# Moving softmax steps and weight preparation around two products with values in a gated cross-attention block

## The chip, the cores and the metric

The kernel runs on one core of one Trainium2 chip, in one launch. The metric is the time of the execution on the device in microseconds (us); of several executions the median is taken. Each core has a matrix engine (PE, with its weight loads shown apart as PEld), a vector engine (DVE), a scalar engine (ACT), a general engine (POOL), and a sync engine (SP), which here issues the DMA transfers. Each engine works through its own list of instructions in order, and waits at an instruction whose inputs or buffers are not ready.

## The reference

```
h   = layernorm(x)                           # x: 32 batches x 64 tokens x 512
q   = h   @ Wq ; k = ctx @ Wk ; v = ctx @ Wv # 32 heads of 128 columns each
s   = q k^T / sqrt(128) + bias               # per batch and head, 64 x 64
p   = softmax(where(mask, s, -inf)), 0 where masked
x   = x + tanh(g_xattn) * ((p v) @ Wo)
y   = layernorm(x) @ weight^T + bffn + (low-rank adapter of the batch's segment)
out = x + tanh(g_ffn) * y
```

All inputs and the output are 32-bit floats.

## The kernel before

**Precision.** A product of 32-bit matrices is made of three matmuls in a reduced 32-bit type: each operand is split into a high part (a cast on ACT) and a low part (the original minus the high part, a subtraction on DVE or POOL), and high x high, high x low and low x high are summed in PSUM (`mm3`, L94 to L100). Every operand of such a product therefore costs a cast and a subtraction before PE can take it. In the attention, `ch` and `cl` (for two of the pairs `cx`) are the high and low part of the context, the attention's weighted sum of values.

**Projections.** Keys, values and queries are made by `unit`: each operand is cut into 2 x 2 blocks and the product is done with seven block products instead of eight (Strassen's method in Winograd's form). The weights' sums of blocks and their splits are made ahead of time by `prep` (with `pair_blocks`). For one pair of heads `prep` has eight steps (the list `PREP`): four sums on POOL (`s1` to `s4`, L283), seven casts on ACT (`hp1` to `hp7`, L290), and seven subtractions on POOL (`lp1` to `lp7`, L294). With the last step it issues on SP the fetch of the next pair's raw weights into the one buffer `rawq` (L259), which has to wait until the last reader of that buffer, the subtraction `lp4`, is done.

**Stages.** The tokens are worked in two phases of 1024 (16 batches). Each phase first makes the keys and values of all heads and puts them into DRAM, and then goes through 16 pairs of heads, numbered n from 0 to 15. For each pair there are these steps, whose order `run` writes out by hand:

- `q_unit(n)`: the query projection, from the prepared weights of pair n.
- `score(n)`: `scores` makes both heads' scores (L861 on PE), adds the bias and takes the row maximum on DVE (L863, L865), subtracts it on POOL (L866), and leaves the exponential (L875) to ACT.
- the softmax's rest, in small steps: sums and reciprocals on DVE, the product with them on POOL (L888), a transpose of 32 x 32 blocks on DVE (`tp`, L899), and copies of these blocks to their places on ACT (L896; `pt`, for pair 14 `pz`). `turned` has them for one pair, `last_turned`, with 16 steps, for pairs 14 and 15 together. The mask is added to the bias ahead of time on POOL (L815).
- `pv(n)`: the product with the values (L1010 on PE) and the split of its result, for each of two heads in two halves: a cast on ACT (L1014) and a subtraction on DVE (L1015), four pairs of them in all.
- `oproj(n)` (for the last pairs `oproj2`): the product of the context with the output weights, `pa` on PE, added to `acc` on DVE (L1059). The output weights are fetched and split like the others (`start_o`, L91).

**What sets the order.** The schedule is manual: each engine gets its instructions in the order in which the program writes them. Everything that isn't a step of `run` is a generator in the list `streams`: the preparation of weights, the softmax's steps, the loads. A call of `beat()` advances every generator in the list by one step. Beats stand in the middle of the large steps: one after each of the seven block products of `unit`, one after each of the four casts and subtractions of `pv`, one after each head's scores, one after each of the eight tiles of `oproj`. So what is issued between two instructions of a large step depends on which generators are in the list at that time.

**Around the change.** Pair 0's product with values comes after `q_unit(1)`; the preparation of pair 2's query weights (`start_q(2)`) is put into the list just before it:

```
q_unit(1)
start_q(2)
pv(0)
score(1)
oproj(0)
q_unit(2)
```

Pair 13's product with values comes right after the scores of pairs 14 and 15, whose `last_turned` is then in the list. Its context goes to the buffers `cx`, and its output projection follows.

Of the kernel before, what the change touches and what calls it, by code (L numbers as in the profile page):

```python
# [27 lines left out]
NPR = H // 2  # L28
# [15 lines left out]
def flamingo_block(ctx: ExitStack, tc: tile.TileContext, x, xT, ctxT, bias, mask, gx, gf,  # L44
# [19 lines left out]
    def beat():  # L64
        for g in list(streams):
            if next(g, True):
                streams.remove(g)

    def drain(g):
        if g is not None and g in streams:  # L70
            streams.remove(g)
            for _ in g:
                pass
# [12 lines left out]
    def psum(name, shape=(P, 512)):  # L86
        return psp.tile(list(shape), F32, tag="ps", name=name)
# [166 lines left out]
    def fetch(kind, n, tag, pieces=1):  # L254
        raw = rwp.tile([P, 1024], F32, tag=tag, name=f"raw{kind}{n}")
        w = 1024 // pieces
        for i in range(pieces):
            sl = slice(i * w, (i + 1) * w)
            nc.sync.dma_start(out=raw[:, sl], in_={"k": wk, "q": wq, "o": wo}[kind][n % NPR][:, sl])  # L259
        raw_of[kind, n] = raw  # L260
# [39 lines left out]
    def prep(kind, n, eng, wait=0, at=0, then=None):  # L300
        for _ in range(wait if at == 0 else 0):
            yield
        do = pair_blocks(kind, n, eng)
        for k, ops in enumerate(PREP):
            if at and k == at:
                for _ in range(wait):
                    yield
            do(*ops)
            if then and k == len(PREP) - 1:
                then()  # L310
            yield
# [483 lines left out]
    def attention(p, res, rest, qt, freed):  # L795
# [6 lines left out]
        def load_v(n):  # L802
            b["v", n] = big(res[3 if n < NPR - 1 else 2], [P, NT, 256], F32, f"v{p}_{n}")
            nc.sync.dma_start(out=b["v", n], in_=vd[p][n // 2][:, :, n % 2 * 256:(n % 2 + 1) * 256])
# [177 lines left out]
        def ctx_of(n):  # L982
            if n in (NPR - 3, NPR - 1):
                if not more_ctx:
                    more_ctx.extend(big(qt[4 + k], [P, 2, TP], F32R, f"cx{p}_{k}") for k in range(2))
                return more_ctx
            return ch, cl

        def turn_pair(n, **pace):
            drain(b["n", n])  # L990
            b["s", n] = turned(n, **pace)
            next(b["s", n])
            next(b["s", n])

        def pv(n, cs=(0, 1)):
            drain(b["s", n])
            if n == NPR - 4:
                turn_pair(n + 1, pace=(0, 1, 2, 2, 3, 2, 2, 2, 2))
                next(b["s", n + 1])


            pt, v, (hi, lo) = pts[n == NPR - 2], b["v", n], ctx_of(n)
            ts = [c * 4 + t for c in cs for t in range(4)]
            for i in (1, 0) if n == 0 else (0, 1):
                ps = [psum(f"po{p}_{n}_{i}_{cs[0]}{h}", (P, len(ts), S)) for h in range(2)]
                for k, t in enumerate(ts):
                    for h in range(2):
                        keys = slice(h * S, (h + 1) * S)
                        for d in range(0, P, S):
                            nc.tensor.matmul(ps[h][d:d + S, k, :], v[keys, t, i * P + d:i * P + d + S],  # L1010
                                             pt[keys, i, t, :], start=True, stop=True)
                for h in range(2):
                    o, l = [x[:, i].rearrange("p (t h s) -> p h t s", h=2, s=S)[:, h, ts[0]:ts[-1] + 1] for x in (hi, lo)]
                    nc.scalar.copy(o, ps[h])  # L1014
                    nc.vector.tensor_tensor(l, ps[h], o.bitcast(F32), ALU.subtract)  # L1015
                    beat()
            if n + 1 < NPR - 1:
                load_v(n + 1)
                if ("n", n + 1) in b:
                    if n != NPR - 4:  # L1020
                        turn_pair(n + 1)
                    streams.append(b["s", n + 1])
# [69 lines left out]
        def run(xq, prefetch, before_last, last_unit, values_read, beside=None):  # L1092
            qb = {}


            def start_q(n, eng=nc.gpsimd, wait=0):
                g = p * NPR + n
                qb[n] = prep("q", g, eng, wait, then=(lambda: fetch("q", g + 1, "r0")) if n + 1 < NPR else None)
                streams.append(qb[n])

            def q_unit(n):
                g = p * NPR + n
                drain(qb.get(n))
                if n == 0:
                    start_q(1, nc.vector, 2)
                elif n == NPR - 1:
                    before_last()
                elif n % 2 == 0 or n == 3:
                    start_q(n + 1)
                qT[n] = kqp.tile([P, 2, TP], F32, tag="kq", name=f"qT{g}")  # L1110
                if n == 1:
                    start_o(0, 2)
                end = unit(wt[("q", g)], xq, None, k_dst(qT[n]), f"q{g}", tuple(carry))
                carry.clear()
                end()
                if n % 2 and 3 < n < NPR - 1:
                    start_q(n + 1)

            def score(*ns):
                for n in ns:  # L1120
                    drain(b.get(("m", n)))
                for n in ns:
                    for i in (0, 1) if n else (1, 0):
                        scores(n, i, qT[n], b["k", n])
                for n in ns:
                    if 0 < n < NPR - 2:
                        load_k(n + 2)
                n = ns[0]
                if n == 0:
                    b["s", n] = first_softmax()  # L1130
                elif n == NPR - 2:
                    b["s", n] = b["s", n + 1] = last_turned()
                else:
                    b["s", n] = both(normed(n, 1), turned(n))
                streams.append(b["s", n])
                if 1 < n < NPR - 2:
                    b["n", n + 1] = normed(n + 1, 5)
                    streams.append(b["n", n + 1])

            q_unit(0)  # L1140
            enter_late()
            b["m", 1] = bias_mask(1)
            score(0)
            streams.append(b["m", 1])
            streams.append(load_acc())
            q_unit(1)
            start_q(2)
            pv(0)
            score(1)
            oproj(0)  # L1150
            q_unit(2)
            start_o(1)
            pv(1)
            q_unit(3)
            score(2, 3)
            for a in range(4, NPR, 2):
                oproj(a - 3)
                q_unit(a)
                start_o(a - 2)
                pv(a - 2)  # L1160
                q_unit(a + 1)
                if a < NPR - 2:
                    oproj(a - 2)
                start_o(a - 1)
                if a < NPR - 2:
                    pv(a - 1)
                else:
                    drain(b["s", a - 1])
                    next(ob[a - 1])
                    held = list(streams)  # L1170
                    streams.clear()
                score(a, a + 1)
                if a == NPR - 8:
                    streams.append(paced(prefetch(), 4))

            n = NPR - 4
            load_v(n + 3)
            beat()
            streams.append(ob[n + 1])
            drain(ob[n + 1])  # L1180

            def between():
                pv(n + 1)
                streams.extend(g for g in held if g is not ob[n + 1])
                last_unit()
                start_o(n + 2, 3)

            def hold():
                drain(ob[n + 3])
                drain(b["s", n + 3])  # L1190
                held[:] = streams
                streams.clear()


            oproj2(n, [(0, 0), (0, 1), between, (0, 2), (0, 3), (1, 0), (1, 1), (1, 2), (1, 3),
                       lambda: start_o(n + 3, 3)]
                   + [(k, t) for t in range(4, NT - 1) for k in range(2)]
                   + [(0, NT - 1), hold, lambda: pv(n + 2), (1, NT - 1), lambda: pv(n + 3)])
            streams.extend(held)
            values_read(acc)  # L1200
            oproj2(n + 2, [(0, 0), (0, 1), (1, 0), (1, 1)] + [(k, t) for t in range(2, NT) for k in range(2)], beside)
# [263 lines left out]
```

## Time and profile before

| | |
|---|---|
| median of 3 runs | 1477.29 us (1476.85 to 1477.81) |
| the profiled execution's own time | 1477.5 us |
| its span in the profile | 1475.7 us |
| granted clock of PE | 1.0 |
| instructions | 31292 |
| PE busy | 99% of the span |
| POOL busy | 71% |
| DVE busy | 64% |
| ACT busy | 48% |
| mean traffic with memory | 176 GB/s |

The profile shows one execution. The shares are of the whole span, so they say which engine is always at work, and not where it waits. Waits are read from the list of what an engine waited for, and from the timeline, where each line is a run of like instructions: start, busy time, engine, line of the program, operation, what is written and read, and in brackets the idle time before it, with what ended it.

### The profile page before, as it was taken

What the parts mean: (1) busy time and instruction counts of PE and PEld (TensorE: products, weight loads), DVE (VectorE), ACT (ScalarE), POOL (GpSimd) and SP (SyncE); (2) the same over time, 40 slices, a digit from 0 to 9 for tenths busy, and PEclk for the clock granted to TensorE, in tenths of its full rate; (3) what the DMA queues carried; (4) which work ended last, traced back from release to release, by engine and by line L of the source; (5) the groups of instructions that cost most, each with busy time, mean ns of one, the idle gap of its engine ahead of it and who ended that gap; (6) DMA issues with size and microseconds to landing.
All of it is one profiled execution on the core that took longest, in us unless ns stands there. A gap on an engine that the chain in (4) does not pass through costs nothing.

```text
span 1475.7 us, 31292 instructions
## 1 busy us (share of the span) xinstructions
PE 1467.0 (99%) x12008; PEld 1220.4 (83%) x12008; DVE 940.2 (64%) x1589; ACT 714.6 (48%) x1582; POOL 1052.0 (71%) x1160
## 2 busy tenths in 40 slices
PE   9999999999999999999999999999999999999999
PEld 7888888888888888888888888888888888888887
DVE  5675464367675677576479756435767567757774
ACT  5444233346555665666334423334655665566611
POOL 4999378969767676767989938896875758577520
PEclk9999999999999999999999999999999999999999
DMA  5754554475443455353385765437545344625554
GB/s 194 287 204 164 179 179 174 143 261 185 152 168 106 168 180 208 101 186 109 127 294 203 235 226 186 173 136 260 184 152 178 103 170 170 217 93 184 136 127 131
DMA packets 148343, 259.38 MB, mean 176 GB/s; under 512 B 44417, under 2 KB 78209, under 8 KB 144098
## 3 DMA queue, kind: packets, MB, share of 16 engines
q1 hardware_dynamic: 147906, 256.87, 50.7%
q8 instruction: 94, 1.54, 0.4%
q10 hardware_dynamic: 288, 0.52, 0.1%
q14 instruction: 55, 0.45, 0.1%
HBM read 179.74 MB, written 77.61 MB: 174 GB/s over the span
## 4 chain that ended last, share of the span: by engine, by line
PE 97%; DVE 1%; issue 1%; ACT 1%; POOL 0%; DMA 0%; SPq 0%; DVEq 0%; POOLq 0%
PE pa L100 23%; PE pxq L100 6%; PE pvq L100 6%; PE pvv L100 6%; PE pxv L100 6%; PE pzv L100 6%; PE pzq L100 6%; PE pzk L100 6%; PE pvk L100 6%; PE pxk L100 6%; PE po L1010 4%; PE ps L861 4%; PE pf L100 3%; PE pyq L100 3%; PE pyv L100 3%; PE pyk L100 3%
## 5 line engine op out<-in xcount | busy, mean ns | idle before, releaser
L100 PE MATMUL pa<-wo,ch 128*128 128x512 f32 x896 | 278.2, 392 | 0.4 <-ACT ch L1014 0.4
L896 ACT COPY pt<-tp 32x256 f32<-32x256 f32 x452 | 182.4, 404 | 69.7 <-DVE tp L899 60.1
L100 PEld LDWEIGHTS pa<-wo,ch 128*128 128x128 f32 x896 | 166.6, 188 | 36.0 <-ACT ch L1014 0.7
L100 PE MATMUL pa<-wo,cl 128*128 128x512 f32 x448 | 174.1, 389 | 0.0
L1059 DVE TENSOR_TENSOR acc<-pa,acc 128x512 f32<-128x512 f32 x192 | 129.4, 681 | 53.5 <-PE pa L100 53.5
L815 POOL TENSOR_TENSOR sm<-sm,madd 128x512 f32<-128x512 f32 x60 | 77.2, 1295 | 96.5 <-DMA sm<-bias 96.5
L888 POOL TENSOR_TENSOR sm<-sm,r 128x512 f32<-128x512 f32 x64 | 66.8, 1044 | 72.5 <-DVE r L887 70.2
L351 DVE TENSOR_TENSOR vt<-pvv,vt 128x512 f32<-128x512 f32 x64 | 44.2, 691 | 103.1 <-PE pvv L100 103.1
L1015 DVE TENSOR_TENSOR cl<-po,ch 128x512 fp32r<-128x512 f32 x112 | 74.5, 689 | 47.6 <-ACT ch L1014 47.2
L100 PEld LDWEIGHTS pa<-wo,cl 128*128 128x128 f32 x448 | 84.1, 188 | 17.7
L866 POOL TENSOR_TENSOR sm<-sm,mx 128x512 f32<-128x512 f32 x64 | 67.0, 1050 | 34.9 <-DVE mx L865 34.7
L351 DVE TENSOR_TENSOR qT<-pvq,qT 128x512 f32<-128x512 f32 x64 | 44.1, 690 | 61.9 <-PE pvq L100 60.5
L373 ACT COPY vt<-pxv 128x512 f32<-128x512 f32 x32 | 18.8, 588 | 130.9 <-PE pxv L100 130.9
L875 ACT ACTIVATE sm<-sm 128x512 f32<-128x512 f32 x62 | 39.2, 633 | 78.0 <-POOL sm L866 78.0
L351 DVE TENSOR_TENSOR kT<-pvk,kT 128x512 f32<-128x512 f32 x60 | 41.1, 684 | 54.8 <-PE pvk L100 53.9
L91 POOL TENSOR_TENSOR wo<-rawo,wo 128x512 fp32r<-128x512 f32 x56 | 71.4, 1299 | 3.1 <-ACT wo L90 3.1
L1010 PEld LDWEIGHTS po<-pt,v 64*64 64x64 f32 x3840 | 59.2, 135 | 10.8 <-issue 9.3
L187 POOL TENSOR_TENSOR vs<-wvr,wvr 128x512 f32<-128x512 f32 x24 | 32.1, 1348 | 49.3 <-DMA wvr<-wv 49.3
L861 PE MATMUL ps<-kB,qT 128*64 128x64 f32 x2048 | 65.2, 223 | 2.1 <-issue 2.0
L1014 ACT CAST ch<-po 128x512 fp32r<-128x512 f32 x112 | 63.0, 594 | 7.9 <-PE po L1010 7.8
L861 PEld LDWEIGHTS ps<-kB,qT 128*64 128x64 f32 x2048 | 61.9, 138 | 5.8 <-issue 4.2
L351 DVE TENSOR_TENSOR vt<-pzv,vt 128x512 f32<-128x512 f32 x64 | 44.2, 690 | 34.0 <-PE pzv L100 33.6
(999 smaller groups left out, 3899.2 us busy)
## 6 DMA issues: line engine op xcount, KB each, us to landing
kd<-kT SPq DMA_DIRECT2D x64, 512.0 KB, 3.8
vd<-vt SPq DMA_DIRECT2D x128, 256.0 KB, 2.4
kB<-kd SPq DMA_DIRECT2D x32, 1024.0 KB, 10.6
v<-vd SPq DMA_DIRECT2D x32, 1024.0 KB, 8.0
rawq<-wq SPq DMA_DIRECT2D x32, 512.0 KB, 3.7
sm<-bias SPq DMA_DIRECT2D x64, 256.0 KB, 5.4
rawo<-wo SPq DMA_DIRECT2D x32, 512.0 KB, 3.7
rawk<-wk SPq DMA_DIRECT2D x31, 512.0 KB, 5.3
```

Of the source, the lines that this page charges most:

```text
L91: eng.tensor_tensor(lo, raw, hi.bitcast(F32), ALU.subtract)
L100: nc.tensor.matmul(ps, a, b, start=start and i == 0, stop=stop and i == len(todo) - 1, skip_group_check=True)
L351: nc.vector.tensor_tensor(o, ps, i, ALU.add)
L815: nc.gpsimd.tensor_tensor(t, t, masks[p][0], ALU.add)
L861: nc.tensor.matmul(ps[h * S:(h + 1) * S, t, :], qT[:, i, tok], kT[:, i, tok], start=True, stop=True)
L866: nc.gpsimd.tensor_tensor(s, s, mx.unsqueeze(2).to_broadcast([P, NT, S]), ALU.subtract)
L888: nc.gpsimd.tensor_tensor(t, t, r.unsqueeze(2).to_broadcast([P, NT, S]), ALU.mult)
L896: f(pts[n == NPR - 2][dst, i, :, qi * 32:(qi + 1) * 32], of[src, :, ki * 32:(ki + 1) * 32])
L1010: nc.tensor.matmul(ps[h][d:d + S, k, :], v[keys, t, i * P + d:i * P + d + S], pt[keys, i, t, :], start=True, stop=True)
L1014: nc.scalar.copy(o, ps[h])
L1015: nc.vector.tensor_tensor(l, ps[h], o.bitcast(F32), ALU.subtract)
L1059: nc.vector.tensor_tensor(acc[t], ps, acc[t], ALU.add)
```

## The change

Two places change. In `pv`, for pair 13 alone, the four beats no longer stand between the four casts and subtractions; all four come after them. In `run`, `start_q(2)` comes after `pv(0)` instead of before it, so that the four beats of `pv(0)` find no preparation of query weights in the list; its eight steps are taken at the beats of `score(1)` (two) and `oproj(0)` (eight, of which six are needed). Both places are passed once in each phase.

```diff
@@ pv @@
                     nc.scalar.copy(o, ps[h])
                     nc.vector.tensor_tensor(l, ps[h], o.bitcast(F32), ALU.subtract)
-                    beat()
+                    if n != NPR - 3:
+                        beat()
+
+            for _ in range(4 if n == NPR - 3 else 0):
+                beat()
             if n + 1 < NPR - 1:
                 load_v(n + 1)
@@ run @@
             q_unit(1)
+            pv(0)
             start_q(2)
-            pv(0)
             score(1)
             oproj(0)
             q_unit(2)
```

## The prediction

> **What bounds the kernel now.** I read the page first (busy shares, clock, chain), then the list of what TensorE (PE) waited for, then the order of time around the two places that the change touches, and last the transfers. Times are us from the span's start.
>
> ```profile
> PE 1467.0 (99%) x12008; PEld 1220.4 (83%) x12008; DVE 940.2 (64%) x1589; ACT 714.6 (48%) x1582; POOL 1052.0 (71%) x1160
> ...
> PEclk9999999999999999999999999999999999999999
> ...
> PE 97%; DVE 1%; issue 1%; ACT 1%; POOL 0%; DMA 0%; SPq 0%; DVEq 0%; POOLq 0%
> ```
>
> PE is busy for 1467.0 of 1475.7 us at full clock, and 97% of the chain is PE's. So a change of order can win only the few us in which PE stands, and it loses what it makes PE stand anew. Where PE stands now:
>
> ```profile
> PE ps L861 <- issue: 2.0, 4, 0.8
> ...
> PE pa L100 <- DVE cx L1015: 1.1, 2, 0.8
> ...
> PE pa L100 <- ACT ch L1014: 0.4, 2, 0.2
> ```
>
> Columns: sum, times, longest. The second row is pair 13 (once per phase), the third is pair 0 (once per phase): exactly the two places of the change. All that it can win is near 1.5 us, plus what a restart costs. The first place, in phase 1 (DVE and PE in order of time; a bracket is the idle time before, and what ended it):
>
> ```profile
> 1370.79 0.71 DVE L899 STREAM_TRANSPOSE tp<-sm 128x512 f32<-128x512 f32 x1 [1.10 <-POOL sm L888]
> 1371.42 0.65 DVE L1015 TENSOR_TENSOR cx<-po,cx 128x512 fp32r<-128x512 f32 x1
> ...
> 1372.13 4.62 PE L100 MATMUL pa<-wo,cx 128*128 128x512 f32 x19 [0.82 <-DVE cx L1015]
> ```
>
> VectorE (DVE) stands 1.10 us for POOL before pair 14's second transpose, the last subtraction of pair 13 is queued behind it, and PE waits 0.82 us. The second place, in phase 0, and what follows from it on POOL, SP, ACT and PE:
>
> ```profile
> 337.00 0.76 POOL L283 TENSOR_TENSOR wsq<-rawq 128x256 f32<-128x256 f32 x1
> 337.43 2.92 DVE L1015 TENSOR_TENSOR cl<-po,ch 128x512 fp32r<-128x512 f32 x4
> 339.03 0.59 ACT L1014 CAST ch<-po 128x512 fp32r<-128x512 f32 x1
> 339.68 1.19 PE L100 MATMUL pa<-wo,ch 128*128 128x512 f32 x4 [0.21 <-ACT ch L1014]
> 342.00 1.05 POOL L866 TENSOR_TENSOR sm<-sm,mx 128x512 f32<-128x512 f32 x1
> 346.17 0.33 SPq L259 DMA_DIRECT2D rawq<-wq  x1
> 352.66 0.74 POOL L283 TENSOR_TENSOR wsq<-rawq 128x256 f32<-128x256 f32 x1 [2.34 <-DMA rawq<-wq]
> 358.04 0.41 ACT L290 CAST wq3p<-wsq 128x256 fp32r<-128x256 f32 x1 [0.21 <-POOL wsq L283]
> 358.94 0.82 ACT L896 COPY pt<-tp 32x256 f32<-32x256 f32 x2
> 360.30 2.09 PE L1010 MATMUL po<-pt,v 64*64 64x64 f32 x128
> 363.44 0.33 SPq L259 DMA_DIRECT2D rawq<-wq  x1
> 367.21 0.74 POOL L283 TENSOR_TENSOR wsq<-rawq 128x256 f32<-128x256 f32 x1 [0.59 <-DMA rawq<-wq]
> ```
>
> Here runs the chain that matters: pair 2's weights are worked on POOL from 337.0, when the last but one of their low parts is done the next raw weights (pair 3) are sent for at 346.17, POOL stands 2.34 us for them, then ACT's casts wait for POOL's sums, and the copies that pair 1's product with values needs (L896, at 358.94) stand behind those casts on ACT. PE takes the first head at 360.30 and the second at 360.30 + 1.05 = 361.35; the copies end at 359.76. The slack is only 1.6 us (the same rows in phase 1, 702.35 us later: copies end at 1062.94, second head at 1063.70, slack 0.8).
>
> **Part A: pair 13's beats after all four heads.** No instruction is added or removed. The only order that changes is DVE's: pair 14's two transposes come after the third and fourth subtraction. The fourth then ends about 1.2 us earlier by the rows (two heads' worth of 0.6 us instead of a transpose and a wait), near 667.8 and 1369.7, well before PE wants it (669.8, 1371.4). So both waits go: 0.30 us in phase 0 and 0.82 us in phase 1 by the brackets. Measured as the stretch between starts of matmuls over its regular 0.227 us, they are 0.57 and 1.09 us, restart included; I take these: **-1.66 us**. The cost: the first transpose is 1.2 us later, and ACT, which copies without a pause behind it, is 1.2 us later through the softmax of pairs 14 and 15. What hides it: those copies end at 680.5 and 1380.5, and PE's product of pair 14 wants them at 683.8 and 1386.2 (slack 3.4 and 5.7); the casts behind that product keep about 0.6 us before PE wants them in phase 0. If that cover is gone the gain is lost, and part A is worth 0.
>
> **Part B: start of pair 2's query weights behind pair 0's product with values.** What is moved is all that the preparation issues: on ACT seven casts (four of them stood between pair 0's four casts), on POOL thirteen operations, on SP the fetch of pair 3's weights. PE's and DVE's orders stay.
>
> - Removed: ACT's four casts of pair 0 follow one another at 0.49 us and end near 338.9, before PE wants them (339.4). That takes away 0.21 us by the bracket, 0.28 us by the starts, per phase. It counts only if nothing later on PE ends at a fixed time; the next wait does, so the gain is swallowed.
> - POOL: before, seven weight operations filled 337.0 to 342.0. Now POOL's first operation is the subtraction of pair 1's maximum (L866). It waits for DVE: four subtractions 0.60 apart from 337.43, then pair 1's scores at 339.84 and the maximum, ended at 341.24. So POOL stands from 337.06 to 341.31, and all weights are queued behind it. From there to the second last low part: four operations of 1.00 (two L866, two L888), nine of 0.70, one of 0.74 = 11.04, ending at 352.35 instead of 346.15: 6.2 us later.
> - Pair 2's own weights are not late: PE takes blocks between 350.5 and 358, and each is made 4 to 5 us before (the first at 346.2). No cost; the cover is pair 0's output projection, 11 us on PE.
> - SP: the fetch waits for that low part, so it is issued at 352.38 instead of 346.17. Behind it on SP stand pair 3's two bias loads (L808); they would land near 356.5, and POOL asks for them near 359.6: no cost.
> - Landing: the fetch of before took 6.35 us (7.20 in phase 1), because the queues were full. The transfers, by stretch (window, length, busy time of PE, PEld, DVE, ACT, POOL, clock, DMA share, GB/s):
>
> ```profile
> 345.00:348.00 3.00, 3.00 (x15) 2.47 (x14) 2.90 (x7) 0.42 (x1) 2.85 (x4) 1.00 1.09 391
> ...
> 354.00:356.00 2.00, 2.00 (x11) 1.65 (x10) 1.06 (x2) 1.91 (x6) 2.00 (x3) 1.00 0.00 0
> ```
>
> ```profile
> DMA to landing us min/median/max: 3.5/3.7/7.2
> ```
>
> At 352.38 the queues have run empty, so the nearest row is the fetch of 363.44: landed 3.64 us later. Two bias loads of 256 KB issued 0.4 us behind it may share its last third of a us; bounds 3.5 (the least of all) and 4.0, taken **3.85**: landing at 356.23 instead of 352.53. A rule speaks to this: the Trainium skill, "DMA: Bandwidth & Descriptors", section "Anatomy of one DMA — SWDGE (gpsimd) path", fits a transfer as 2.0 us plus its bytes over 436e3, 3.2 us for these 512 KB. It was fitted on another issuing path and lies under the least value of this trace; by it the new wait would be 0.65 us shorter per phase (sum +1.4 instead of +2.7). The row decides.
> - From landing to PE: POOL starts 0.13 after landing, and the five operations up to the sum that ACT needs end 5.35 us later in both phases (352.66 to 358.01); from there the last two copies end 1.75 us later (358.01 to 359.76). So 356.23 + 0.13 + 5.35 + 1.75 + 0.05 = 363.51 for PE's second head, instead of 361.35: **+2.2 us** of a new wait in phase 0. Phase 1 has the same absolute chain, since there too the landing follows POOL's end, not the full queue: 1065.86 against 1063.70, +2.2. Sum of B: +4.4.
> - What is late next: pair 3's weights (the second block near 365.1, PE at 366: margin 0.9), the fetch for pair 4 (367.2 instead of 363.44, over 10 us of slack), the softmax of pairs 2 and 3 (about 1 us later, 3 us of slack). Each costed at nothing; if the 0.9 fails, a few tenths per phase.
>
> A second rule bears on the new wait. In the trace the longest stand of PE here is 0.82 us with the clock at 1.00. The Trainium skill, "TensorE: Matmul & The Clock Gate", Part 1, section on what is actually happening, says that a free-running window of about 3.4 us without work halves PE's clock for as long. A stand of 2.2 us is below it: nothing by row or rule. In the first rival below it would not be.
>
> **Sum.** -1.66 + 4.4 = +2.7 us. The profiled execution (1477.5, span 1475.7) becomes about 1480.2; it lies 0.2 over the median of 1477.29, so the median becomes **1480.0**. A measurement of this kernel tells apart about 0.2%, 2.95 us: the forecast lies just inside. Each 0.1 us of landing moves it by 0.2.
>
> **The rivals.**
> - Slower, by a slow landing: the moved fetch takes what it took before (6.35 and 7.20 us) though the queue is empty. Then PE waits 4.7 and 5.5 us, sum +8.5: 1485.8, and up to 1.7 us more per phase by the clock rule. The place is the same second head; beyond a landing of 3.97 us the change leaves the 0.2% band. For it: two of the 32 fetches took that long, at this very place. Against: the share of 0.00 at 354 to 356.
> - Slower, by A's lost cover: the late copies of pairs 14 and 15 make PE wait as long as before. +4.4: 1481.7. Against: slack of 3.4 and 5.7 us.
> - No new wait: POOL's work from landing to the sum shrinks (part of the mask additions between could be done by then), so that ACT is in time. Then -1.66 - 0.56 = -2.2: 1475.1, still inside 0.2%. Against: 5.35 us in both phases, whose order doesn't change.
> - The change doesn't do what it says: DVE's late subtraction hangs on pair 13's own casts, not on the transpose, and B's order changes little; 1477.3. Against: the bracket on the transpose, released by POOL.
>
> **How the numbers follow.** Forecast 0.62 (1478.6 to 1481.2 by itself; 0.36 of it inside the band, 0.26 beyond), slow landing 0.14, lost cover 0.10, no new wait 0.10 (0.06 inside, 0.04 faster), not as it says 0.04. So slower 0.50, same 0.46, faster 0.04. The range 1477.2 to 1483.2 takes in the forecast, the lost cover, the last rival and a landing of up to 5 us; it leaves out most of the slow landing and of the case without a wait.
>
> **What would show it.** Right: no wait of pa on cx or ch in PE's list, in their place about 2.1 us, twice, of po (L1010) on ACT's pt copies near 363.5 and 1065; the fetch issued at 352.4 and landed under 4 us later; POOL idle about 4.2 us before 341.3. Wrong: no wait of po; the fetch landing over 6 us later; a new wait at 684 to 690.

## The result, and the profile after

| | before | after |
|---|---|---|
| median | 1477.87 us (16 runs) | 1481.50 us (16 runs) |
| lowest to highest | 1476.08 to 1479.26 | 1478.74 to 1482.69 |
| ratio, 95% interval | | 1.0023 (1.0016 to 1.0030) |
| span of the profiled execution | 1475.7 | 1480.1 |
| mean granted clock of PE in it | 1.000 | 0.999 |

The change costs 3.6 us (2.4 to 4.4 by the interval); +2.7 were predicted. The forecast's sums for the two parts nearly hold, and one term was missing altogether. The page of the changed kernel first:

```profile
PE 1469.2 (99%) x12008; PEld 1222.9 (83%) x12008; DVE 942.0 (64%) x1589; ACT 714.3 (48%) x1582; POOL 1051.3 (71%) x1160
...
PEclk9999999999999999999999999999999999999999
```

It says almost nothing: PE is busy 2.2 us longer with the same matmuls. Busy time that grows without more work is a first hint at the clock, but the row of the clock shows all nines, because a slice is 37 us long. The list of PE's waits says more:

```profile
PE po L1010 <- ACT pt L896: 3.9, 2, 2.0
PE ps L861 <- issue: 1.5, 4, 0.5
```

The waits of pa on cx and on ch are gone, and po waits for the copies twice, 2.0 us at most, as forecast. The chain that leads there, in order of time (POOL, SP, ACT, PE; the bracket is the idle time before):

```profile
341.49 1.04 POOL L866 TENSOR_TENSOR sm<-sm,mx 128x512 f32<-128x512 f32 x1 [4.24 <-DVE mx L865]
...
352.54 0.33 SPq L259 DMA_DIRECT2D rawq<-wq  x1
...
356.32 0.74 POOL L283 TENSOR_TENSOR wsq<-rawq 128x256 f32<-128x256 f32 x1 [1.86 <-DMA rawq<-wq]
...
361.67 0.41 ACT L290 CAST wq3p<-wsq 128x256 fp32r<-128x256 f32 x1 [1.38 <-POOL wsq L283]
361.98 0.58 ACT L373 COPY qT<-pxq 128x512 f32<-128x512 f32 x1
...
362.57 0.81 ACT L896 COPY pt<-tp 32x256 f32<-32x256 f32 x2
...
363.44 1.15 PE L1010 MATMUL po<-pt,v 64*64 64x64 f32 x60 [1.96 <-ACT pt L896]
```

POOL stands 4.24 us for pair 1's maximum, the fetch for pair 3 goes out at 352.54 instead of 346.17, POOL starts on it 3.78 us after that issue, ACT's cast waits 1.38 us for POOL's sum, the last copies are queued behind this cast, and PE takes the second head at 363.44. The other place, in phase 1: DVE's four subtractions stand in one block, the transposes behind them, and PE goes on without a bracket:

```profile
1373.05 2.48 DVE L1015 TENSOR_TENSOR cx<-po,cx 128x512 fp32r<-128x512 f32 x4
1375.45 0.70 DVE L899 STREAM_TRANSPOSE tp<-sm 128x512 f32<-128x512 f32 x1
...
1375.86 5.60 PE L100 MATMUL pa<-wo,cx 128*128 128x512 f32 x24
```

PE's order is the same in both kernels, so the start of every matmul can be set against its counterpart, and the difference shows where it changes: 0.27 and 0.28 us won before pair 0's projection, 2.18 and 2.17 lost at pair 1's second head, 0.58 and 1.17 won at pair 13. That is +2.05 us. But in phase 0 the matmuls right after the stand lose another 1.7 us, with no wait in any list. The stretches around the stand, phase 0 (window, length, busy time of PE, PEld, DVE, ACT, POOL, each with the number of instructions that touch the window, then granted clock, DMA share, GB/s), show why:

```profile
361.00:364.00 3.00, 1.04 (x68) 0.91 (x61) 0.01 (x1) 2.28 (x6) 3.00 (x4) 1.00 0.02 5
364.00:365.00 1.00, 1.00 (x41) 0.83 (x31) 0.00 (x0) 0.85 (x3) 1.00 (x3) 0.87 0.00 0
365.00:368.00 3.00, 3.00 (x9) 2.33 (x8) 2.18 (x4) 3.00 (x7) 3.00 (x5) 0.50 0.04 5
368.00:370.00 2.00, 2.00 (x10) 1.67 (x9) 1.18 (x2) 0.14 (x1) 2.00 (x2) 0.96 0.67 250
```

PE is busy throughout from 365 to 368, but at half the clock: nine matmuls touch these 3 us, where 14 do at full clock (in the run with eight added matmuls, below). The half clock begins after the stand, at 364.73, and lasts 3.41 us. Phase 1, behind an equal stand (1.93 us), shows nothing of it:

```profile
1070.00:1074.00 4.00, 4.00 (x54) 3.36 (x44) 2.18 (x4) 3.85 (x9) 4.00 (x7) 1.00 0.00 0
```

Of the 16 executions of the changed kernel, three have a mean clock of 1.000 and take 1478.74 to 1479.18 us; the other 13 have 0.999 or less and take 1480.36 to 1482.69. Of the kernel before, all 39, 31 and 41 executions beside the three sets of experiments below had 1.000. The three at 1.000 lie only 0.9 to 1.3 us over the median of the kernel before, less than the 2.0 us that the places cost in the profile; they are few, and the stands of executions without a profile are not on record.

The theory now: the places cost +2.0 us (2.7 were forecast); the stands that the second part makes are long enough to halve PE's clock in part of the cases, which costs another 1.6 us in the mean. The rival: the places are all that is due to the change, and the halved clock was an accident of that execution.

### The profile page after: what moved, and what is told of

Its sections match the earlier page's. It is cut to its first block, busy times and chain, and to the rows that moved or that the text cites. A ratio compares the mean times of both kernels' runs of the same rounds, so it can differ in the third digit from the quotient of the medians.

```text
span 1480.1 us, 31294 instructions
## 1 busy us (share of the span) xinstructions
PE 1469.2 (99%) x12008; PEld 1222.9 (83%) x12008; DVE 942.0 (64%) x1589; ACT 714.3 (48%) x1582; POOL 1051.3 (71%) x1160
## 4 chain that ended last, share of the span: by engine, by line
PE 93%; POOL 4%; issue 1%; DVE 1%; ACT 1%; DMA 0%; POOLq 0%
PE pa L100 21%; PE pvv L100 6%; PE pzv L100 6%; PE pxv L100 6%; PE pxq L100 5%; PE pvk L100 5%; PE pzk L100 5%; PE pxk L100 5%; PE pvq L100 5%; PE pzq L100 5%; PE po L1010 4%; PE ps L861 4%; PE pf L100 3%; PE pyv L100 3%; PE pyk L100 3%; PE pyq L100 3%
## 5 line engine op out<-in xcount | busy, mean ns | idle before, releaser
L1010 PE MATMUL po<-pt,v 64*64 64x64 f32 x3840 | 63.7, 220 | 3.9 <-ACT pt L896 3.9
```

## The experiments

### Each part alone

The first part alone (pair 13's beats after all four heads, pair 2's weights where they were):

```diff
-                    beat()
+                    if n != NPR - 3:
+                        beat()
+            for _ in range(4 if n == NPR - 3 else 0):
+                beat()
```

> Only the pair 13 part of the change. If the waits of PE on cx (0.57 and 1.09 us, restart included) are worth what their places show, -1.7 us against the kernel before, no wait of pa on cx in PE's list, granted clock 1.000. If the later transposes are paid for again by the copies of pairs 14 and 15, about 0 and a new wait between 683 and 690.

Measured: 1475.80 us against 1477.80, ratio 0.9985 (0.9977 to 0.9993), clock 1.000 in all 14 executions; pa waits for cx no more, and there is no wait between 683 and 690. By the starts of matmuls 0.52 and 1.07 us are won at the two places. The gain is real, and it is not paid for later.

The second part alone:

```diff
-            start_q(2)
             pv(0)
+            start_q(2)
```

> Only the pair 0 part of the change. By the places alone (two stands of PE of about 2.0 us less 0.27 saved before each) +3.8 us. If such a stand also makes the clock of PE fall to one half for about 3.4 us afterwards, in one of the two phases in the mean, as in the profile of the changed kernel, +5.4 us and a granted clock of 0.999 or less in most executions. If the halved clock was a chance of that one execution, +3.8 and 1.000.

Measured: 1483.36 us, ratio 1.0038 (1.0026 to 1.0051): +5.6 us. The clock was 0.999 or 0.998 in all five executions. In the profiled one both stands (2.15 and 1.93 us) are followed by the half clock; the stretches of phase 1:

```profile
1071.00:1072.00 1.00, 1.00 (x4) 0.79 (x5) 0.40 (x1) 1.00 (x4) 1.00 (x3) 0.72 0.00 0
1072.00:1074.00 2.00, 2.00 (x6) 1.60 (x5) 1.38 (x3) 2.00 (x6) 2.00 (x4) 0.50 0.00 0
1074.00:1075.00 1.00, 1.00 (x4) 0.76 (x3) 0.90 (x2) 0.55 (x2) 1.00 (x2) 0.58 0.54 98
1075.00:1077.00 2.00, 2.00 (x11) 1.60 (x10) 0.74 (x2) 0.00 (x0) 1.60 (x2) 1.00 0.55 213
```

The two medians' differences, -2.0 and +5.6, add up to +3.6, what the whole change cost in the result above (the whole was not run beside them, and on another chip it cost 5.4, below). The rival's +3.8 for this part lies at the lower end of the interval; the clocks speak against it.

### Is it the copies' place behind the cast?

To the changed kernel, the last two copies of pair 1 one beat earlier:

```diff
-                    b["s", n] = both(normed(n, 1), turned(n))
+                    b["s", n] = both(normed(n, 1), turned(n, pace=(1, 2, 2, 3, 2, 2, 4) if n == 1
+                                                       else (1, 2, 2, 3, 2, 2, 2, 2)))
```

> The changed kernel, with the last two block copies of pair 1 issued one beat earlier, ahead of the cast that waits for POOL's fourth sum. If the stand of PE is the copies' wait behind that cast, as the chain in the prediction has it, the wait of po on pt is gone; next late is pair 3's second block of weights, for which PE then stands 0.9 us or less per phase: -1.7 - 0.5 + up to 1.8, so about -0.4 us against the kernel before, clock 1.000. If PE stands for another reason (values, transposes), +3.6 as in the changed kernel.

Measured: 1477.72 us, ratio 0.9999 (0.9991 to 1.0007), clock 1.000 in all 13 executions. One line moved by one beat gives back all that the change had cost. ACT now makes the copies ahead of the cast, and PE waits for pair 3's second block of weights instead (timeline, then PE's waits):

```profile
359.77 1.64 ACT L896 COPY pt<-tp 32x256 f32<-32x256 f32 x4
...
361.96 0.41 ACT L290 CAST wq3p<-wsq 128x256 fp32r<-128x256 f32 x1 [0.55 <-POOL wsq L283]
...
365.30 0.96 PE L100 MATMUL pyq<-x0p,wq3p 128*128 128x512 f32 x3 [0.56 <-POOL wq3p L294]
```

```profile
PE pyq L100 <- POOL wq19p L294: 0.6, 1, 0.6
PE pyq L100 <- POOL wq3p L294: 0.6, 1, 0.6
```

So the stand of 2 us was the copies' wait behind a cast that waits for POOL. The weights themselves, some 3.7 us late, cost 0.6 us per phase when nothing else hangs on them.

### Does the stand halve the clock?

To the changed kernel, matmuls whose result is overwritten, put where PE stands:

```diff
                 ps = [psum(f"po{p}_{n}_{i}_{cs[0]}{h}", (P, len(ts), S)) for h in range(2)]
+                if n == 1 and i == 1:
+                    for _ in range(8):
+                        nc.tensor.matmul(ps[0].rearrange("p a b -> p (a b)"), hi[:, 1, 0:P],
+                                         hi[:, 1, 0:512], start=True, stop=True, skip_group_check=True)
```

> The changed kernel with eight more matmuls of 128x512 (8 x 0.227 = 1.8 us) on PE just where it stands, before the second head of pair 1's product with values; their result is overwritten. They fit into the stand of 2.0 us. If the halved clock after the stand is what the prediction lacked, the stand shrinks to 0.2 to 0.4 us, the clock is 1.000 in all executions, and the time is about +2.0 us against the kernel before (the places alone), some 1.6 us under the changed kernel, though PE has 3.6 us more to do. If the halving has nothing to do with the stand, +3.6 as in the changed kernel, or more by what does not fit.

Measured: 1481.14 against 1478.78 us, ratio 1.0015 (1.0008 to 1.0022): +2.4 us, and the clock is 1.000 in all 19 executions. The stand is 0.19 and 0.42 us, and the stretch that ran at half clock before now runs at full:

```profile
PE po L1014 <- ACT pt L896: 0.6, 2, 0.4
```

```profile
361.00:364.00 3.00, 2.81 (x44) 1.99 (x40) 0.00 (x0) 2.06 (x6) 3.00 (x5) 1.00 0.03 5
364.00:365.00 1.00, 1.00 (x55) 0.93 (x46) 0.00 (x0) 0.82 (x4) 1.00 (x2) 1.00 0.00 0
365.00:368.00 3.00, 3.00 (x14) 2.43 (x14) 1.92 (x3) 3.00 (x7) 3.00 (x6) 1.00 0.00 0
```

Against 0.50 and nine matmuls in the same window of the changed kernel. But the interval touches that of the changed kernel, which was not run beside it, so both were run once more side by side, with three matmuls in place of eight as a third:

> The changed kernel itself, beside the two next ones on one chip: +3.6 us, of which +2.0 are the places and +1.6 the halved clock; a clock of 1.000 in a few executions only, and these 1.7 us faster for each halving that they lack.

> The changed kernel with the eight matmuls in the stand once more, now beside it on the same chip. If the halving follows from the stand: 1.3 to 1.6 us under the changed kernel and clock 1.000 throughout. If the lower time of the first run was the other chip's: no difference between the two.

> The same with three matmuls (0.7 us), which leave a stand of about 1.3 us. If a stand of 1.3 us is short enough (that of 1.7 us in the run with four more operations on POOL had no halving, those of 1.9 us had it three times in four): as with eight, clock 1.000. If what counts is the share of work in a stretch and not the longest stand, it may still be halved in some executions, and the time lies between.

| kernel, on one chip (before: 1478.58 us) | median | ratio (95%) | executions below clock 1.000 |
|---|---|---|---|
| changed | 1483.97 | 1.0038 (1.0024 to 1.0052) | 5 of 5 |
| with three matmuls in the stand | 1481.04 | 1.0022 (1.0016 to 1.0029) | 5 of 21 |
| with eight | 1481.66 | 1.0019 (1.0012 to 1.0025) | 0 of 21 |

The changed kernel is the slowest though it has the least to do. Its interval still touches that of the kernel with eight, but of those 21 executions only one (1484.17 us) is above its quickest (1483.35). It lost more than expected here (+5.4 where +3.6 was written): in the profile its stands are longer, 2.22 and 2.58 us, since the fetch took longer (POOL starts 4.05 us after its issue in phase 0, not 3.78), and four of its five executions have a clock of 0.998, which is two halved stretches and not one (each takes 0.0012 of the mean clock). With three matmuls the stand is 1.4 to 1.8 us and the halving comes seldom: the sixteen executions at 1.000 take 1480.20 to 1482.78 us, the five others 1484.22 to 1484.99. Three of these five have a clock of 0.999, one halved stretch, and lie 3.4 to 3.9 us over the median of the sixteen, more than its 1.7 us; whether their stands were longer is not on record.

### How long must a stand be?

To the kernel before, more work on POOL between the landing of pair 3's weights and the copies (k = 2, 4, 6):

```diff
+                    for _ in range(k if (kind, n % NPR, q) == ("q", 3, "s3") else 0):
+                        eng.tensor_tensor(s3, a11, a21, ALU.subtract)
```

> The kernel before, with pair 3's first sum of weights done three times instead of once on POOL: two more operations of 0.70 us between the landing of the weights and the copies that PE waits for. By the slack read from the profile (1.6 us in phase 0, 0.8 in phase 1) PE stands 0 and 0.6 us: +0.6 us, clock 1.000.

> The same with four more operations: stands of 1.2 and 2.0 us: +3.2 us by the stands alone. If a stand of 2 us halves the clock in half of the cases, and one of 1.2 us does not, +4 us and a clock of 0.999 in about half of the executions.

> The same with six more operations: stands of 2.6 and 3.4 us: +6.0 us by the stands alone, clock 1.000, if only a whole window of 3.4 us without work halves the clock (then hardly any here). If a stand of 2 us is enough, both stands are followed by 3.4 us at half clock, +9.4 us and a clock of 0.998 or less.

| k | stands, phase 0 and 1 | median against 1478.78 | ratio (95%) | executions below clock 1.000 |
|---|---|---|---|---|
| 2 | none, 0.67 | 1479.84 | 1.0006 (0.9998 to 1.0015) | 0 of 12 |
| 4 | 2.40, 1.69 | 1486.63 | 1.0056 (1.0042 to 1.0071) | 4 of 4 |
| 6 | 3.35, 3.09 | 1490.84 | 1.0082 (1.0069 to 1.0096) | 4 of 4 |

PE's waits in the profiles of k = 4 and k = 6:

```profile
PE po L1012 <- ACT pt L898: 4.1, 2, 2.4
```

```profile
PE po L1012 <- ACT pt L898: 6.4, 2, 3.3
```

The expectations for k = 4 and k = 6 missed: +7.9 and +12.1 us, not +4 and +9.4. Three reasons show in the profiles. The repeated operations took 0.82 us each and not 0.70 (four of them from 353.30 to 356.57). The fetch did not land as in the profile of before (6.35 and 7.20 us after its issue) but, for k = 4, after 7.3 and 6.6 us. The two together make the stands 2.40 and 1.69 us and not 1.2 and 2.0. And the half clock came, in phase 0 for k = 4 and in both phases for k = 6:

```profile
365.00:367.00 2.00, 2.00 (x15) 1.59 (x9) 1.27 (x2) 2.00 (x5) 2.00 (x4) 0.50 0.00 0
1070.00:1074.00 4.00, 3.81 (x72) 3.25 (x73) 1.43 (x3) 3.84 (x10) 4.00 (x7) 1.00 0.00 0
```

That is k = 4: half clock behind the stand of 2.40, full clock behind that of 1.69. For k = 6 the clock of phase 1 falls at 1072.52, before the stand has ended, and stays at half to 1079.34, twice as long as elsewhere. For k = 4 the profiled execution was the quickest of the four (1484.53 of 1484.53 to 1489.95), so the median holds more than the profile explains. The other three have clocks of 0.999, 0.998 and 0.996, so two of them had more than one halved stretch; the rest is open.

All stands of these profiles in one row: none of those up to 1.78 us (0.2 to 0.7, 1.38, 1.69, 1.78) was followed by the half clock; of 1.93, 1.93, 1.96, 2.15 and 2.22 three were (one of the two of 1.93, 1.96, 2.15); 2.40, 2.58, 3.09 and 3.35 all were.

The length alone does not sort them, but the clock rows do. In each of the thirteen profiles every change of the clock lies a whole number of windows of 3.413 us from the others (the two halvings of the second part alone begin at 364.88 and 1071.44, 207 windows apart; so do those of k = 6), and a halved stretch is one such window, or two. The two stands of the changed kernel, cut along this grid:

```profile
361.32:364.73 3.41, 1.45 (x69) 1.25 (x64) 0.00 (x0) 2.86 (x8) 3.41 (x5) 1.00 0.02 5
364.73:368.14 3.41, 3.41 (x9) 2.64 (x9) 2.32 (x4) 3.41 (x7) 3.41 (x6) 0.50 0.06 13
...
1064.47:1067.88 3.41, 3.04 (x77) 2.32 (x75) 1.38 (x2) 1.57 (x5) 3.41 (x5) 1.00 0.03 7
1067.88:1071.29 3.41, 1.85 (x63) 1.69 (x64) 0.10 (x1) 3.21 (x9) 3.41 (x5) 1.00 0.00 0
1071.29:1074.70 3.41, 3.41 (x16) 2.82 (x15) 2.78 (x5) 2.86 (x6) 3.41 (x5) 1.00 0.19 50
```

The stand of 1.96 us lies within one window (1.45 us of work in 3.41), and the next window runs at half clock. That of 1.93 us is divided between two, 0.37 and 1.56 us, and the clock stays full. In the thirteen profiles, while the clock is full and the kernel runs, seven windows have 1.81 us or more without work on PE (1.81, 1.96, 2.04, 2.13, 2.40, 2.58, 3.00), and after each of them the clock is halved; the next lower have 1.69, 1.64, 1.56 and 1.50 us, and after none of them it is. So in these runs it is the time without work within one window that counts, with a limit between 1.69 and 1.81 us. The stand of 2.22 us was spared because it was divided into 0.58 and 1.64.

### A version that beats both

The first part's device for pair 0 too, instead of the second part: `start_q(2)` stays ahead of `pv(0)`, and the beats of pair 0 come after all four heads.

```diff
-                    beat()
+                    if n not in (0, NPR - 3):
+                        beat()
+            for _ in range(4 if n in (0, NPR - 3) else 0):
+                beat()
```

> The preparation stays before pair 0's product with values, but pair 0 gets what pair 13 gets: its four beats after all four casts and subtractions. ACT's casts of pair 0 then follow one another, while POOL still works on pair 2's weights before it works on the scores. If the loss of the change lies in POOL's order alone, -1.7 - 0.5 = -2.2 us and a clock of 1.000. Rival: POOL's first low part waits about 0.8 us for its cast, the fetch is 0.8 us later, and PE stands in phase 1, where there was 0.8 us of slack: -1.7 or a little less.

Measured: 1475.44 us against 1477.80, ratio 0.9983 (0.9976 to 0.9990), clock 1.000 in all 18 executions: it is faster than the kernel before and 6 us under the changed one (by the difference of the differences, -2.4 and +3.6). POOL's weights do wait for their cast, and the fetch is 0.8 us later than before, at 346.94:

```profile
339.27 0.73 POOL L294 TENSOR_TENSOR wq2p<-rawq,wq2p 128x256 fp32r<-128x256 f32 x1 [0.54 <-ACT wq2p L290]
...
346.94 0.33 SPq L259 DMA_DIRECT2D rawq<-wq  x1
```

But pair 1's second head does not wait, so this was within the slack. Its gain over the first part alone (2.4 to 2.0 us) is within the intervals; that it is better is not shown.

## Why the prediction was right or wrong

- **First part.** Right. 0.57 and 1.09 us were read as stretches between starts; 0.58 and 1.17 showed in the changed kernel, 0.52 and 1.07 with this part alone, whose median fell by 2.0 for a forecast of 1.66. The later copies of pairs 14 and 15 made nobody wait.
- **Second part, the chain.** Right link by link: POOL's start at 341.49 (forecast 341.31), the fetch at 352.54 (352.38), the second head at 363.44 (363.51). The landing was mis-sized a little: 3.85 us were taken for fear of the bias loads behind it, and POOL began 3.78 us after the issue, where landing plus start would have been 3.98; the row of 3.64 was the better value. The stand by starts was 2.18, and the 0.27 won before it is part of it, so that gain was swallowed as forecast; the loss left is 1.9 per phase and not 2.2, of which the shorter landing is 0.2.
- **The step that failed: "nothing by row or rule".** The prediction held the new stand of 2.2 us to be harmless to the clock, since the longest stand at these places was 0.82 us at full clock, and since the Trainium skill's page "TensorE: Matmul & The Clock Gate" (Part 1, "What's actually happening") speaks of an idle window of about 3.4 us. The row did not reach that far, and the rule does not hold as the prediction read it: 1.81 us without work in a window were enough, and stands of 1.93 to 2.22 us were followed by the half clock three times in five. The page's free-running window itself agrees with the grid of 3.413 us and with the halved stretch of 3.41 us. Its price was named (1.7 us), but only for the first rival. An estimate with it: at 0.0012 of the mean clock for each, the clocks of the 16 executions come to 18 halved stretches, 1.1 per execution and 1.9 us; with the 2.05 of the places that is 3.9, against 3.6 measured (2.4 to 4.4).
- **The two misses worked against each other**: the places cost 0.7 us less than forecast, the clock 1.6 to 1.9 us more than nothing. That +3.6 still lies in the forecast's own +1.3 to +3.9 (1478.6 to 1481.2 over 1477.29) is therefore partly luck, and does not show that its sum was right.
- **The rivals.** Slow landing, lost cover and no new wait are all refuted by the list of PE's waits and by the experiments. The one rival that was true in part was not on the list as such: a stand that costs more than its length.
- **What is late next.** The margin of 0.9 us for pair 3's second block held: no wait on it in the changed kernel. It became the wait as soon as the copies were out of the way (0.6 us).

## What to carry to other kernels

When a change trades several short stands of PE for one longer one, look at the longest stand by itself: the second part alone made two stands of 2 us, and cost 5.6 us, since half clock of 3.4 us came behind them, 1.7 us each time in its profile. Here a stand above some 1.7 us ran this risk, more so the longer it was. Read the clock from narrow windows around the stand and from the clocks of all executions, since a page with 40 slices cannot show 3 us at half speed. When a late transfer makes an engine late, see what is queued behind the instruction that waits: moving the two copies ahead of the waiting cast gave back the whole loss.

## What had not been expected of the hardware

The half clock after a stand of only 2 us, told above, and that two stands of 1.93 us go different ways by their place on the grid of 3.413 us. The grid lies differently against the kernel from execution to execution (the changed kernel's two profiles have edges at 364.73 and at 1069.03, no whole number of windows apart); no run here sets its place.

The other surprise is at the start of phase 1, which the change does not touch. DVE's two subtractions of c1p took 1.70 and 1.77 us in the profile of before, and 1.22 and 5.59 us in that of the changed kernel. In both POOL makes two subtractions of c1p beside them, which took 3.43 us together before and 2.56 us in the changed kernel. The changed kernel's:

```profile
L91 DVE TENSOR_TENSOR c1p<-c,c1p x2: 1218/3406/5594, 714.9 to 720.4; 128x512 fp32r<-128x512 f32 x2
```

PE then waits 0.8 us (1.35 by the starts). The same wait of PE stands in the profiles of k = 2 and k = 6, which have nothing of the change, and not in that of the kernel with the early copies, so it isn't the change's; it is one reason why the spans of the two profiled executions are 4.4 us apart where the medians are 3.6 apart. What decides between the two was not tried.
